# A gated stage stretched over ten and a half images of a deformable stage, with the preparation of the last images moved and compressed

## Chip, core and metric

The kernel runs on one core of one Trainium2 chip. The metric is the device time of one execution in microseconds (us). Three runs of the kernel before gave a median of 13687.8 us (13683.05 to 13691.02).

## What is computed

The input is 32 images of 128 channels on a 32 x 32 grid, in fp32. Two residual layers follow each other. Cut to what matters:

```python
# layer 0: state-space layer with a gate, on group-normalised x
h = einsum('bdl,de->ble', u, W_enc) + b_enc            # 128 -> 1024 features
y = causal_convolution(h, K) + D * h                   # K has 64 taps per feature
y = gelu(y)
g = y @ W_glu + b_glu                                  # 1024 -> 2048
g = g[..., :1024] * sigmoid(g[..., 1024:])
out = layernorm(h + g) @ W_dec + b_dec                 # 1024 -> 128
x = x + out
# layer 1: deformable 8 x 8 depthwise convolution, on group-normalised x
off = depthwise_conv3x3(x, offset_w) + offset_b        # 64 taps, 2 offsets each
for tap in 64 taps:                                    # bilinear sampling at moved places
    acc += weight[tap] * sample(x, place(tap) + off[tap])
x = x + gelu(batchnorm(acc))
```

The gate `g` of layer 0 and its decoding are called the gated part here, layer 1 the deformable part. An image needs both, in this order.

## The kernel before

`main_block` (L518) runs after the convolution of layer 0, whose result for all images lies in DRAM. It is a list of instructions written out in order for every engine: under `tc.manual_schedule()` each engine and each DMA queue works through its own list in the order in which the Python code issues the instructions.

**Gated part.** `first_part(b)` (L718) is a generator. For each image it runs two halves of 512 columns; in each half, for each of eight feature blocks m, TensorE makes the gate (L729, eight matmuls), the value (L752, eight) and the residual `gph` (L768, one), and decodes the block before it (L657). It yields 863 after every matmul, 292 times an image. ScalarE (ACT) takes the gate out of PSUM with a sigmoid (L736) and squares the result (L789); VectorE (DVE) adds bias and multiplies (L760, L781); GpSimd (POOL) sums (L659, L790). `close` (L674) spreads the layer norm of a half over the next fifteen yields, by `later` and `tick`, and ends with the store of the image's half to `x1_d`. Gate, value and residual share three PSUM buffers.

**Deformable part.** `second_part(b)` (L1039) runs 17 packs of columns, each in four pieces; a piece has three matmuls `dps` (L1063), so an image has 204. The count of an image's matmuls, 0 to 203, is called its slot here. DVE takes each matmul out of PSUM times the weights (L1066, four PSUM buffers); POOL adds the product up (L1077, L1082). The matmul's moving operand is `ds` times `dhy` (L1020 in `weights`, two pieces ahead). Both are loaded from DRAM by the SyncE (SP) queue (`load_hat`, L988, up to five and six pieces ahead), out of tables of "hats" max(0, 1 - |rel - k|). For the last two images (`ALONE = B - 2`) only a quarter of each `ds` is loaded, and ACT copies it to the other partitions (L1012 in `spread_fine`, three pieces ahead); DVE also takes half of the first additions from POOL there (L1077).

**Preparation.** `prepare(b)` (L805) returns the steps that make the tables of image b, each with the slot of image b - 1 at which `second_part` issues it: `fetch` 28 (SP loads the stored `x1_d`), `total` 35, `mean` 37, `variance` 40 and `normal` 42 (group norm, with two small matmuls in TensorE's list and a square root on ACT), nine `taps` of the 3 x 3 convolution at 44 to 68 on DVE, `turn` 47 and 50 (transposes), `largest` 71, `across` 74 and `down` 79 on DVE, `spread` 81 and 82 (eight SP DMAs each to a DRAM scratch), `gather` 89 and 90 (an SP load back, each), and 24 `hat` steps from 96 to 174: two ACT activations (L925, L926) on one of two `hat` buffers and a store of 312 KB from ACT's queue (L927). `ready` at 178 only makes the tables known to Python. The first load of the next image's tables is issued at slot 186.

**Order.** `run_along` (L505) merges generators so that they advance in proportion to the totals given with them: it always takes the next item of the one whose share of its total is smallest. Gated image b + 2 is merged with deformable image b for b = 0 to 29; deformable images 30 and 31 have no gated part beside them.

Of the kernel before, what the change touches and what calls it, by code (L numbers as in the profile page):

```python
# [15 lines left out]
B, C, H, W = 32, 128, 32, 32  # L16
# [445 lines left out]
PIECES = 8 // KY2  # L462
# [15 lines left out]
def span_of(u):  # L478

    j0, j1 = max(0, 7 - u), min(7, NU - 1 - u) + 1  # L480
    return j0, j1 - j0


def rows_of(piece):

    a, b = 15 - KY2 * piece, 23 - KY2 * piece
    return (0, a), (a, b - a), (b, H - b)
# [17 lines left out]
def run_along(*streams):  # L505


    left = [[gen, float(total), 0.0] for gen, total in streams]
    while left:
        s = min(left, key=lambda e: e[2] / e[1])  # L510
        cost = next(s[0], None)
        if cost is None:
            left.remove(s)
        else:
            s[2] += cost


def main_block(nc, tc, const, ins, x, u_d, y_d, x1_d, out, offmax):  # L518
# [16 lines left out]
    T = 512  # L535
    YB = 11
    ALONE = B - 2
    SB, HB = 5, 4
    ctx = ExitStack()
    with ctx:  # L540
# [55 lines left out]
        for k in range(KD):  # L596
            nc.tensor.matmul(
                fold[:, 0:1], w_dec[:, k, :], beta[:, k : k + 1],
                start=(k == 0), stop=(k == KD - 1),
# [19 lines left out]
        for i in range(2):  # L619
            t = dram1.tile([2, NCOL], F32, tag=f"rel_d{i}", name=f"rel_d{i}")  # L620
            flat = t.rearrange("a (p l) -> (a p) l", p=P // 2)
            n = 2 * NCOL // P
# [177 lines left out]
        FIRST = 2 * (KD * (2 * KD + 2) + 2) * MM  # L800
# [1 line left out]

        images = {}

        def prepare(b):  # L805

            st = {}

# [34 lines left out]
            def taps(lo, hi):  # L843
                def run():
                    if lo == 0:
                        st["co"] = two.tile([P, L], F32, tag="img", name=f"dco_{b}")
                    co3 = st["co"].rearrange("p (h w) -> p h w", w=W)
                    v3 = st["v"].rearrange("p (h w) -> p h w", w=W)
                    for n in (4, 0, 1, 2, 3, 5, 6, 7, 8)[lo:hi]:
                        dy, dx = n // 3 - 1, n % 3 - 1  # L850
                        y0, y1 = max(0, -dy), H - max(0, dy)
                        x0, x1 = max(0, -dx), W - max(0, dx)
                        src = v3[:, y0 + dy : y1 + dy, x0 + dx : x1 + dx]
                        to = co3[:, y0:y1, x0:x1]
                        wn = off_w[:, n : n + 1]
                        if n == 4:
                            nc.vector.tensor_scalar(
                                to, src, wn, off_b, op0=ALU.mult, op1=ALU.add
                            )
                        else:  # L860
                            nc.vector.scalar_tensor_tensor(
                                to, src, wn, to, op0=ALU.mult, op1=ALU.add
                            )

                return run
# [88 lines left out]
            def ready():  # L954
                images[b] = st["vt_d"], [st["h0"], st["h1"]]

            steps = [
                (28, fetch), (35, total), (37, mean), (40, variance), (42, normal),
                *((44 + 3 * i, taps(i, i + 1)) for i in range(9)),
                (47, turn(0)), (50, turn(1)),  # L960
                (71, largest), (74, across), (79, down), (81, spread(0)), (82, spread(1)),
                (89, gather(0)), (90, gather(1)),
                *((96 + 82 * i // len(hats), step) for i, step in enumerate(hats)),
                (178, ready),
            ]
            return steps

        NP = len(PACKS)
        pieces = [(b, n, i) for b in range(B) for n in range(NP) for i in range(PIECES)]
# [2 lines left out]
        def slots_of(n):  # L972
            return sum(span_of(u)[1] for u in PACKS[n][1])

        def runs_of(n):

            runs, slot = [], 0
            for u in PACKS[n][1]:
                j0, nj = span_of(u)
                first = u * 8 + j0  # L980
                if runs and first == runs[-1][0] + runs[-1][2]:
                    runs[-1][2] += nj
                else:
                    runs.append([first, slot, nj])
                slot += nj
            return runs

        def load_hat(k, a):  # L988
# [7 lines left out]
            else:  # L996
                t = hy_of[k] = hypool.tile([P, 16, KY2, H], F32, tag="hy", name=f"dhy_{k}")
            rows = 4 if a == 0 and b >= ALONE else 16
            for first, slot, m in runs_of(n):
# [6 lines left out]
        def spread_fine(k):  # L1006

            if k >= len(pieces) or pieces[k][0] < ALONE:
                return
# [13 lines left out]
        def windows(b, n):  # L1023

            if n == NP:
                b, n = b + 1, 0
            x0 = PACKS[n][0]
            if b == B or (n > 0 and PACKS[n - 1][0] == x0):
                return
            t = xw_of[b, x0] = three.tile(  # L1030
                [P, len(YWINDOWS), C], F32, tag="xw", name=f"dxw_{b}_{x0}"
            )
            for j, y0 in enumerate(YWINDOWS):
                nc.sync.dma_start(
                    t[:, j, :],
                    at(images[b][0], (y0 * W + x0) * C, [[W * C, 16], [C, 8], [1, C]]),
                )

        def second_part(b, steps):  # L1039


            steps = sorted([*steps, *ending], key=lambda e: e[0])
            ending.clear()
            acc = one.tile([P, W, H], F32, tag="acc", name=f"dacc_{b}")
            nc.gpsimd.memset(acc, 0.0)
            for n in range(NP):
                x0, us = PACKS[n]
                m = slots_of(n)
                xw = xw_of[b, x0]
                windows(b, n + 1)  # L1050
                for i in range(PIECES):
                    k = (b * NP + n) * PIECES + i
                    s = s_of.pop(k)
                    w = wk[:, table_of[n] : table_of[n] + m, KY2 * i : KY2 * (i + 1)]
                    prod = ppool.tile([P, 16, KY2, H], F32, tag="prod", name=f"dp_{k}")
                    for j, (y0, ny) in enumerate(rows_of(i)):
                        while steps and steps[0][0] <= 3 * (PIECES * n + i) + j:
                            steps.pop(0)[1]()
                        ps = psam.tile([P, 512], F32, tag="sam", name=f"dps_{k}_{j}")
                        ps = ps[:, : m * KY2 * ny].rearrange(  # L1060
                            "p (s k y) -> p s k y", s=m, k=KY2
                        )
                        nc.tensor.matmul(  # L1063
                            ps, xw[:, j, :], s[:, :m, :, y0 : y0 + ny], start=True, stop=True
                        )
                        nc.vector.tensor_mul(  # L1066
                            prod[:, :m, :, y0 : y0 + ny],
                            ps,
                            w[:, :, :, None].to_broadcast([P, m, KY2, ny]),
                        )  # L1070
                        if j == 0:
                            weights(k + 2)
                            spread_fine(k + 3)
                        yield measure(m * KY2 * ny)
                    load_hat(k + SB, 0)
                    adder = nc.vector if b >= ALONE and i % 2 else nc.gpsimd
                    adder.tensor_add(prod[:, :m, 0], prod[:, :m, 0], prod[:, :m, 1])  # L1077
                    slot = 0
                    for u in us:
                        j0, nj = span_of(u)  # L1080
                        to = acc[:, u - 7 + j0 : u - 7 + j0 + nj]
                        nc.gpsimd.tensor_add(to, to, prod[:, slot : slot + nj, 0])  # L1082
                        slot += nj

            o = two.tile([P, L], F32, tag="img", name=f"do_{b}")
            xr = two.tile([P, L], F32, tag="img", name=f"dxr_{b}")
            nc.sync.dma_start(xr, x1_d[b])
            nc.gpsimd.tensor_scalar(
                o.rearrange("p (h w) -> p w h", w=W), acc, bn_mean, bn_inv,
                op0=ALU.subtract, op1=ALU.mult,  # L1090
            )
            ending.append((6, lambda: nc.scalar.activation(o, o, AF.Gelu, bias=bn_beta)))
            ending.append((11, lambda: nc.vector.tensor_add(o, o, xr)))
            ending.append((14, lambda: nc.scalar.dma_start(out[b], o)))

        ending = []
        def measure(columns):

            return columns + 40.0

        SECOND = sum(
            measure(slots_of(n) * KY2 * ny)
            for n in range(NP) for i in range(PIECES) for _, ny in rows_of(i)
        )
# [16 lines left out]
        ctx.enter_context(tc.manual_schedule())  # L1121
        run_along((first_part(0), FIRST))
        run_along((first_part(1), FIRST), (opening(), 90.0))
        for b in range(B):
            steps = prepare(b + 1) if b + 1 < B else []
            if b + 2 < B:
                run_along(
                    (first_part(b + 2, last=(b + 2 == B - 1)), FIRST),
                    (second_part(b, steps), SECOND),
                )  # L1130
            else:
                run_along((second_part(b, steps), SECOND))
        for _, step in ending:
            step()

# [148 lines left out]
```

## Time and profile before

| what | value |
|---|---|
| median of three runs | 13687.8 us |
| the profiled execution, its own time | 13693.54 us |
| its span, from first to last instruction | 13691.8 us |
| PE busy in the span | 13161.7 us (96%) |
| DVE, POOL, ACT busy | 8807.4 (64%), 9028.9 (66%), 3285.6 us (24%) |
| gated image 0 with nothing beside it | 251.0 us (1577.9 to 1828.9) |
| a deformable image with a gated one beside it | 368.1 us |
| deformable image 30, alone, with the preparation of image 31 | 295.6 us (13139.4 to 13435.0) |
| deformable image 31, alone, with the tail of the kernel | 256.8 us (13435.0 to 13691.8) |

Image boundaries are read from the timeline: a gated image begins with its first L729, a deformable one with the clearing of its accumulator on POOL (L1045). Gated image 31 has its last L729 at 13113.1 us.

The busy shares are means over the whole span. They say little of a single stage, so the stages are asked one by one, with the stretches of the table as windows. A line of such an answer gives the stretch, its length and, for each engine, the busy time and the number of instructions in it, then the granted TensorE clock, the mean busy share of the DMA engines and GB/s.

### The profile page before, as it was taken

To read this page: it belongs to the slowest core of one execution; us is meant where nothing else is said; L and a number is where in the kernel's file an instruction comes from. 1 tells how busy PE (TensorE), PEld (TensorE's weight loads), DVE (VectorE), ACT (ScalarE), POOL (GpSimd) and SP (SyncE) were. 2 spreads that over 40 slices of the span, in tenths; PEclk is the share of its full clock that TensorE was granted. 3 is DMA by queue.
4 is the path that set the end of the run, shared out by engine and by line. 5 is a ranking of instruction groups with operands and counts; after the bars stand their busy time and mean duration, and the time that the engine had idled before them with its cause. 6 is when DMAs were issued, how large, how long until landed. Compare 5 with 4: busy or idle time off the path is not lost.

```text
span 13691.8 us, 134306 instructions
## 1 busy us (share of the span) xinstructions
PE 13161.7 (96%) x40482; PEld 7261.4 (53%) x40482; DVE 8807.4 (64%) x12719; ACT 3285.6 (24%) x4767; POOL 9028.9 (66%) x8834
## 2 busy tenths in 40 slices
PE   7889899999999999999999999999999999999976
PEld 6888645555555555555555555555555555555533
DVE  6777426666666666666666666666666666666677
ACT  4333222121112222222222121222222222222245
POOL 2444216777777777777777777777777777777766
PEclk8999999999999999999999999999999999999988
DMA  6888518888888888888888888888888888888865
GB/s 222 265 259 264 181 57 222 233 230 229 230 233 234 240 235 234 234 233 229 238 239 233 230 230 231 232 232 241 236 234 236 231 231 235 239 237 229 230 197 166
DMA packets 1715628, 3105.79 MB, mean 227 GB/s; under 512 B 308306, under 2 KB 1018322, under 8 KB 1713874
## 3 DMA queue, kind: packets, MB, share of 16 engines
q1 hardware_dynamic: 1502290, 2641.91, 71.9%
q10 hardware_dynamic: 163456, 320.92, 6.5%
q0 software_dynamic: 49152, 134.28, 3.0%
q8 instruction: 329, 5.39, 0.2%
q14 instruction: 401, 3.28, 0.1%
HBM read 2630.36 MB, written 466.06 MB: 226 GB/s over the span
## 4 chain that ended last, share of the span: by engine, by line
PE 80%; DMA 10%; DVE 4%; ACT 2%; POOL 2%; issue 1%; SPq 1%; ACTq 0%; DVEq 0%; POOLq 0%
PE gpv L752 24%; PE gpg L729 24%; PE dps L1063 23%; DMA ds<-dhat 4%; PE gph L768 3%; DMA y_d<-yo 3%; PE gpo L657 3%; PE psz L224 3%; DVE z L231 2%; PE psy L270 2%; DMA dhat<-dh 1%; DVE ds L1020 1%; POOL y_d L303 1%; ACT ds L1012 1%; DMA dhy<-dhat 1%
## 5 line engine op out<-in xcount | busy, mean ns | idle before, releaser
L1066 DVE TENSOR_TENSOR dp<-dps,k_weight_slots 128x256 f32<-128x256 f32 (+17 forms) x6528 | 3081.4, 482 | 3051.3 <-PE dps L1063 2869.6
L1063 PE MATMUL dps<-ds,dxw 128*128 128x256 f32 (+18 forms) x13056 | 4729.4, 448 | 208.3 <-DVE dp L1066 197.6
L1082 POOL TENSOR_TENSOR dacc<-dacc,dp 128x256 f32<-128x256 f32 (+3 forms) x4736 | 4415.1, 932 | 443.2 <-DVE dp L1077 75.6
L1063 PEld LDWEIGHTS dps<-ds,dxw 128*128 128x128 f32 x13056 | 2472.7, 193 | 3221.1 <-issue 2578.0
L729 PE MATMUL gpg<-gy,g_w_glu 128*128 128x512 f32 x8192 | 3987.7, 593 | 22.5 <-DMA gy<-y_d 15.8
L752 PE MATMUL gpv<-gy,g_w_glu 128*128 128x512 f32 x8192 | 3974.5, 592 | 0.0
L1077 POOL TENSOR_TENSOR dp<-dp 128x512 f32<-128x512 f32 (+3 forms) x2108 | 2621.5, 1244 | 1909.4 <-DVE dp L1066 1906.7
L1020 DVE TENSOR_TENSOR ds<-ds,dhy 128x1024 f32<-128x1024 f32 (+3 forms) x2176 | 3152.6, 1449 | 810.9 <-DMA ds<-dhat 659.2
L729 PEld LDWEIGHTS gpg<-gy,g_w_glu 128*128 128x128 f32 x8192 | 1544.7, 190 | 1238.2 <-issue 966.7
L752 PEld LDWEIGHTS gpv<-gy,g_w_glu 128*128 128x128 f32 x8192 | 1548.7, 189 | 1158.3 <-issue 915.4
L790 POOL TENSOR_TENSOR gs<-gs,gq 128x512 f32<-128x512 f32 x448 | 633.8, 1415 | 1343.7 <-ACT gq L789 1343.7
L789 ACT ACTIVATE gq<-gr 128x512 f32<-128x512 f32 x448 | 282.2, 630 | 4648.5 <-DVE gr L781 4564.7
L303 POOL DMA_DIRECT2D y_d<-yo x1024 | 590.5, 584 | 949.4 <-ACT yo L291 820.9
L736 ACT ACTIVATE gs<-gpg,k_b_glu 128x512 f32<-128x512 f32 x512 | 351.9, 687 | 2490.0 <-PE gpg L729 2355.6
L270 PE MATMUL psy<-toe,z 128*128 128x192 f32 x4096 | 718.3, 335 | 102.0 <-ACT yo L291 100.2
L925 ACT ACTIVATE dh<-dr,k_minus 128x624 f32<-128x624 f32 x768 | 621.7, 810 | 648.3 <-DMA dhat<-dh 569.8
L270 PEld LDWEIGHTS psy<-toe,z 128*128 128x128 f32 x4096 | 675.1, 193 | 144.4 <-ACT yo L291 138.9
L282 DVE TENSOR_TENSOR psy<-psy,t 32x256 f32<-32x256 f32 (+1 forms) x1280 | 554.1, 433 | 272.9 <-ACT t L278 241.1
L760 DVE SCALAR_TENSOR_TENSOR gs<-gpv,k_b_glu,gs 128x512 f32<-128x512 f32 x512 | 379.9, 742 | 437.4 <-PE gpv L752 423.5
L224 PE MATMUL psz<-w_enc,u 128*128 128x128 f32 x4096 | 576.8, 296 | 86.4 <-DVE z L231 40.2
L659 POOL TENSOR_TENSOR gs<-gs,gr 128x512 f32<-128x512 f32 x448 | 634.9, 1417 | 0.0
L926 ACT ACTIVATE dh<-dh,one 128x624 f32<-128x624 f32 x768 | 626.2, 815 | 24.9
(162 smaller groups left out, 6091.4 us busy)
## 6 DMA issues: line engine op xcount, KB each, us to landing
dhy<-dhat SPq DMA_DIRECT2D x1536, 512.0 KB
ds<-dhat SPq DMA_DIRECT2D x1440, 512.0 KB
dhat<-dh ACTq DMA_DIRECT2D x768, 312.0 KB
y_d<-yo POOLq DMA_DIRECT2D x1024, 128.0 KB, 5.0
gy<-y_d SPq DMA_DIRECT2D x512, 256.0 KB
u<-u_d SPq DMA_DIRECT2D x224, 512.0 KB
toe<-kp_d SPq DMA_DIRECT2D x128, 768.0 KB
dxw<-dvt_d SPq DMA_DIRECT2D x1248, 64.0 KB
```

The costliest lines, as they stand in the source:

```text
L224: nc.tensor.matmul(ps[:, j, :], u[:, (NB * g + ORDER[j]) * P : (NB * g + ORDER[j] + 1) * P], w_enc[:, k * P : (k + 1) * P], start=True, st ...
L270: nc.tensor.matmul(ps[:, c // 2, c % 2, :], rows[i][:, g * CG + c0 + c, :], toe[:, c0 + c, :], start=True, stop=True,)
L303: nc.gpsimd.dma_start(y_d[d0 : d0 + CG, :, i * NB + ORDER[j], :].rearrange("d b l -> b d l"), yo[i][j * B : (j + 1) * B],)
L659: nc.gpsimd.tensor_add(sums[0], sums[0], r)
L729: nc.tensor.matmul(gate, w_glu[:, k, D + m * P : D + m * P + P], ys[k], start=(k == 0), stop=(k == KD - 1),)
L752: nc.tensor.matmul(val, w_glu[:, k, m * P : m * P + P], ys[k], start=(k == 0), stop=(k == KD - 1),)
L790: nc.gpsimd.tensor_add(sums[1], sums[1], sq)
L1020: nc.vector.tensor_mul(s[:, :m], s[:, :m], hy[:, :m])
L1063: nc.tensor.matmul(ps, xw[:, j, :], s[:, :m, :, y0 : y0 + ny], start=True, stop=True)
L1066: nc.vector.tensor_mul(prod[:, :m, :, y0 : y0 + ny], ps, w[:, :, :, None].to_broadcast([P, m, KY2, ny]),)
L1077: adder.tensor_add(prod[:, :m, 0], prod[:, :m, 0], prod[:, :m, 1])
L1082: nc.gpsimd.tensor_add(to, to, prod[:, slot : slot + nj, 0])
```

## The change

Up to deformable image 19 the order stays as it is, but that the `ready` step, which issues nothing, stands at 184 and not at 178. From deformable image 20 on the ten gated images 22 to 31 are one generator, the deformable images 20 to 31 another, and they are merged so that the ten gated images last as long as ten and a half deformable ones. Gated image b + 2 therefore ends 0.05 images later for each image from 20 on, and gated image 31 ends in the middle of deformable image 30. The preparation of image b + 1 starts later by the same amount, and its steps are drawn together so that they still end at slot 184: of the distance from 184 a step keeps (184 - start) / 156, from 1 for image 21 to 0.346 (start 130) for image 31.

```diff
+    SLOWER = B - 12
+    LONGER = 0.5
+    FETCH, READY = 28, 184
...
-        def prepare(b):
+        def prepare(b, start=FETCH):
...
-                (178, ready),
+                (READY, ready),
             ]
-            return steps
+            stretch = (READY - start) / (READY - FETCH)
+            return [(READY - int((READY - n) * stretch), step) for n, step in steps]
...
-        for b in range(B):
-            steps = prepare(b + 1) if b + 1 < B else []
-            if b + 2 < B:
-                run_along(
-                    (first_part(b + 2, last=(b + 2 == B - 1)), FIRST),
-                    (second_part(b, steps), SECOND),
-                )
-            else:
-                run_along((second_part(b, steps), SECOND))
+        for b in range(SLOWER):
+            run_along(
+                (first_part(b + 2), FIRST), (second_part(b, prepare(b + 1)), SECOND)
+            )
+        n = B - 2 - SLOWER
+        pace = (n + LONGER) / n
+        def firsts():
+            for b in range(SLOWER + 2, B):
+                yield from first_part(b, last=(b == B - 1))
+        def seconds():
+            for b in range(SLOWER, B):
+                steps = []
+                if b + 1 < B:
+                    done = (b - SLOWER) * (pace - 1)
+                    steps = prepare(b + 1, FETCH + int(3 * NP * PIECES * done))
+                yield from second_part(b, steps)
+        run_along((firsts(), n * FIRST), (seconds(), (n + LONGER) * SECOND))
```

More of the change, by code (lines that the diff above doesn't have):

```diff
@@ L957, in prepare @@
             steps = [
-                (28, fetch), (35, total), (37, mean), (40, variance), (42, normal),
+                (FETCH, fetch), (35, total), (37, mean), (40, variance), (42, normal),
                 *((44 + 3 * i, taps(i, i + 1)) for i in range(9)),
```

## The prediction, made before the changed kernel ran

> **What bounds the kernel now.** I read the stages first, because the shares of the whole span hide the end. This is the answer for the gated image 0 alone, deformable image 28 beside gated image 30, the hand-over, and the two images alone.
>
> ```profile
> core 0: us, PE busy (x) PEld busy (x) DVE busy (x) ACT busy (x) POOL busy (x), PEclk, DMA share, GB/s
> 1577.90:1828.90 251.00, 251.00 (x579) 111.00 (x580) 29.30 (x39) 26.24 (x37) 32.36 (x26) 0.99 0.08 28
> 12403.10:12770.50 367.40, 366.17 (x1006) 187.69 (x1005) 235.89 (x336) 77.04 (x103) 266.78 (x246) 1.00 0.87 235
> 13117.70:13139.40 21.70, 16.93 (x39) 8.10 (x37) 9.71 (x14) 7.60 (x9) 15.65 (x17) 0.84 0.33 106
> 13139.40:13435.00 295.60, 192.31 (x427) 94.21 (x428) 225.04 (x331) 183.02 (x197) 183.80 (x185) 0.75 0.64 186
> 13435.00:13691.80 256.80, 158.87 (x397) 79.39 (x395) 210.62 (x307) 130.36 (x131) 189.70 (x184) 0.84 0.58 168
> ```
>
> A merged image is PE from end to end (366.2 of 367.4), so it costs the gated 251.0 plus what the 204 `dps` matmuls need, 368.1 - 251.0 = 117.1 us. Alone, an image takes 256.8 or 295.6 us: there PE waits. The waits of image 30 say for whom, and the costliest groups of that stretch say what ACT and DVE do.
>
> ```profile
> PE dps L1063 <- DVE dp L1066: 88.5, 75, 3.7
> ACT ds L1012 <- DMA ds<-dhat: 86.4, 39, 7.5
> DVE ds L1020 <- ACT ds L1012: 62.9, 39, 5.5
> PE gn_pm L824 <- ACT dv L820: 6.1, 1, 6.1
> ```
>
> ```profile
> L1012 ACT COPY ds<-ds 32x1024 f32<-32x1024 f32 (+7 forms) x138 | 136.2, 987 | 113.2 <-DMA ds<-dhat 86.4 <-PE dps L1063 11.4 <-ACT dh L926 7.5
> L1020 DVE TENSOR_TENSOR ds<-ds,dhy 128x1024 f32<-128x1024 f32 (+3 forms) x70 | 99.1, 1416 | 65.2 <-ACT ds L1012 62.9 <-DMA ds<-dhat 2.2
> ```
>
> PE waits for DVE, and DVE in turn, 62.9 us of image 30, for ACT's copies. In the middle of image 31, with no preparation, DVE is busy nearly without a gap (31.8 of 32.1 us), and a pack takes 14.2 us in its timeline, 1.18 us a slot. In image 30 ACT is nearly full while it makes hats, as its timeline shows: a copy pair of 2.1 us, a hat of 1.6, its issue of 0.33.
>
> ```profile
> 13340.81 0.81 ACT L926 ACTIVATE dh<-dh,one 128x624 f32<-128x624 f32 x1
> 13341.66 0.33 ACTq L927 DMA_DIRECT2D dhat<-dh  x1
> 13342.02 2.12 ACT L1012 COPY ds<-ds 32x1024 f32<-32x1024 f32 x2 [0.40 <-ACT dh L926]
> 13344.17 0.82 ACT L925 ACTIVATE dh<-dr,k_minus 128x624 f32<-128x624 f32 x1
> ```
>
> The other long step is the spread, seen in the SP queue's timeline of image 30:
>
> ```profile
> 13254.21 4.73 SPq L896 DMA_DIRECT2D rel_d<-drel  x8
> ...
> 13259.61 4.36 SPq L896 DMA_DIRECT2D rel_d<-drel  x8
> ...
> 13268.66 0.59 SPq L910 DMA_DIRECT2D dr<-rel_d  x1
> ```
>
> **What the Trainium skill says.** "DMA: Bandwidth & Descriptors", section "Issuing engines are not separate DMA queues": transfers of SP, ACT and POOL run on the same 16 DMA engines and interleave. The trace agrees: in the packets of ACT's queue the last one of a hat ends mostly 1.8 us after the issue in the opening, beside gated image 1, but 2.9 to 6.5 in image 30 and 2.2 to 8.2 in image 25, beside SP's loads. "Perfetto Trace Analysis", section "DMA Instruction — HWDGE (DVE, Sync)": the profiled interval ends when the sequencer is free, the movement is not in it. It agrees too: 0.33 us for L927 against those 1.8 to 8.2. "ScalarE: Activation LUTs", section "What ACT_TABLE_LOAD costs": about 1283 ns a load; the load ahead of the square root (L835) took 1.28 us.
>
> **The change part by part.** The sum is a difference against the profiled execution (13693.5 us, its span 13691.8 and 1.7 around it); I add it to the median, 13687.8, 5.7 below that execution.
>
> *Merged stage.* The gated work is the same. Ten gated images now carry 10.5 deformable ones: 0.5 x 117.1 = **+58.6**. The half image 30 in it brings ACT copies (34 x 2.1 us) and 17 additions of 0.74 us on DVE, in about 184 us where ACT was busy about 38 and DVE about 118: they lie beside PE. If that cover failed, the DVE part would cost at most 12.6.
>
> *Image 30 alone.* Before, image 29's last product was at 13125.5 and image 31's first at 13428.0; less a normal gap of 2.4 that is **-300.1**. It includes about 14 us in which `close` of gated image 31 ran with nothing beside it (DVE waited 6.7 for `gm`, then worked its chain). After, slots 102 to 203 remain: packs 8.5 to 15 at image 31's rate 107.3, the last pack at image 30's own 23.2 (four short runs per table, where SP issues 8 loads of 0.65 us for a piece of 3.6 us), 130.5; and `close`, now between pieces, at DVE's own 7.0 plus a wait, 8. Then the preparation P, wholly in this half, slots 130 to 184:
>
> - DVE work: `normal` 1.3, taps 11.7, `largest` 1.2, `across` 2.1, `down` 1.7, 18.0 in a stage that DVE bounds.
> - The norm chain, `fetch` 130, `total` 133, `mean` 134, `variance` and `normal` 135. Before there were 14 slots. PE stands at `gn_pm` for ACT (6.1 above), with all `dps` behind it, ACT at the fetch, with the copies behind it, and DVE at the square root and its table load. About 6 of DVE idle, 3 more than before.
> - Spread and gather: 16 issues on SP, 10 us, the gather's landing about 16 us after `down`. In slots that is 149 to 154, 6 us. Behind them on SP stand the `ds` and `dhy` loads, behind the waiting hat on ACT the copies. DVE can go on to slot 159 from copies already made, so 5 or 6 us are lost.
> - Hats: slots 154 to 181 hold 24 hats and 9 copy pairs. A hat needs 2.07 us of ACT (back to back in the opening), so 24 x 2.07 + 9 x 2.12 = 69 us, in a stretch of 27 slots, 32 us. From `down` to slot 183: 16 + 69 = 85 against 35 x 1.18 = 41, so 44 with the gather's loss. The buffers are two, so a store landing after 4.5 us makes (2.07 + 4.5) / 2 = 3.3 a hat, 79 in all: +10. SP catches up meanwhile with the last pack's loads, -4. I take 43.
>
> P = 18 + 6 + 43 = **67**. From below: no landing waits, chain at 2, SP's catch-up 8: 53. From above: all stores land late and the chain costs 10: 82. Sum: 130.5 + 8 + 67 = **+205.5**.
>
> *Preparation of images 22 to 30, merged.* A slot is 1.83 us. `ready` costs nothing; all that moves is ACT, DVE, PE and SP items, past each other's neighbours, and what matters is who stands behind. The order of the built kernel has, for image 30's preparation (slots 119 to 184), 12 hats between one gate sigmoid and the next and 10 in the next gap. A gate comes every 23 us; 12 hats need 25 us of ACT with no landing wait, about 35 at 2.9 each. The lag grows to about 26 us. Behind it stand sigmoid and square; the gate's PSUM is needed again after the value's matmuls, 11 us later, and DVE's four buffers and POOL's products give about 4 more. Some 8 us lost, in image 29. The norm chain, taps squeezed from 24 to 10 slots (DVE 60% busy plus 12 us in 18) and the spread with a gather after three slots instead of eight add about 5. Images 28 and 27 are milder (hats every 2.9 and 3.3 us): 3 and 1. Earlier ones keep over 3.6 us a hat: zero. **+17**. From below: such steps already cost about 2 us of PE an image (19.5 of 21.7 in one window of image 25), where the loads of `gy` meet the gather; the shift may part them, -10 in all. From above: 45.
>
> Sum: 58.6 - 300.1 + 205.5 + 17 = **-19**, 13669. Image 31 stays at 256.8, POOL tail included.
>
> **Rivals.**
> - *The squeeze is hidden.* P 55 and no loss in the merged images: 58.6 - 300.1 + 193.5 = -48, **13640**. For it: POOL and DVE have 30% to spare there and the waits named are short. Against: in image 30 the hats and copies alone are 69 us of ACT in 32. Chance 0.30.
> - *A jam at ACT makes it slower.* In image 25 hat stores land after 5 to 8 us beside full loads; two buffers then give 4.5 us a hat, 108 us instead of 59 for image 30's hats. Lag 49, less 15 of slack: 34 lost; for images 29, 28, 27 in the same way 23, 13, 3, and 13 for chains and gathers: 86, so -36 + 86 = +50, **13738**. Place: sigmoids of gated images 29 to 31. It decides from 36 us of loss on. For it: ACT already waits 17 us an image for these stores. Against: the DMA engines are less loaded in packs 12 to 16 (share 0.56 to 0.8), and a stalled PE asks for fewer loads. Chance 0.13.
> - The change does what it says: the built order has the last gated matmul in image 30's middle and image 31's `fetch` after the store.
>
> **Numbers.** The forecast case has 0.57. It covers 13652 to 13690, and about a fifth of it, 0.11, lies below 13660. A measurement of this kernel can tell about 0.2%, 27 us, from no change. Faster: 0.30 + 0.11 = 0.41; within: 0.47; slower: 0.12. All low ends together give 58.6 - 300.1 + 138.5 + 53 - 10 = -60, all high ones 58.6 - 300.1 + 138.5 + 82 + 45 = +24. They will hardly all meet, so the range stops a few us short of both: -53 to +20, 13635 to 13708; the upper end reaches into the jam.
>
> **What would show it.** After: image 30's middle to image 31's first product about 205 us; ACT over 90% busy for 70 us there, L1020 waiting for L1012; merged images 20 to 25 at 374 us each with PE full; in image 29 sigmoids late behind L925, PE idle some 13 us. It is wrong if the hats of image 30 take 100 us, or if PE idles in images 26 to 28.

## The result, and the profile after

The changed kernel takes 13801.5 us (median of four runs, 13796.9 to 13812.6) against 13689.4 for the kernel before in the same comparison. The ratio is 1.0083, with a 95% interval of 1.0066 to 1.0101: it is slower by 112 us. The forecast was 13669, and the range to 13708 misses the time by 93.

The profiled execution took 13796.91 us, its span 13795.1, which is 103.3 more than the span before. Lines have moved by three to five: `dps` L1063 is now L1068, its eviction L1066 is L1071, the copies L1012 are L1017, the hats L925 to L927 are L929 to L931, the sigmoid L736 is L739.

The same table of stages as before (stretch, length, busy time of PE, PEld, DVE, ACT and POOL, the granted clock, DMA share, GB/s), for the deformable images 28 and 29, the first and the second half of image 30, and image 31:

```profile
core 0: us, PE busy (x) PEld busy (x) DVE busy (x) ACT busy (x) POOL busy (x), PEclk, DMA share, GB/s
12364.00:12754.10 390.10, 361.45 (x970) 185.10 (x969) 234.36 (x331) 75.30 (x100) 269.13 (x250) 0.96 0.84 223
12754.10:13139.80 385.70, 365.54 (x984) 187.19 (x983) 232.94 (x331) 80.27 (x103) 261.25 (x236) 0.97 0.81 219
13139.80:13329.20 189.40, 180.85 (x485) 92.44 (x484) 118.59 (x179) 87.20 (x96) 119.84 (x119) 0.97 0.48 131
13329.20:13531.00 201.80, 107.14 (x221) 53.45 (x220) 122.09 (x176) 110.89 (x124) 84.99 (x87) 0.65 0.54 155
13531.00:13795.10 264.10, 159.59 (x405) 79.50 (x403) 214.05 (x313) 134.10 (x135) 197.17 (x189) 0.85 0.58 167
```

Image boundaries here, and in all tables below, are the first eviction L1071 of an image in the timeline. Two things are to be seen. The second half of image 30 took 201.8 us, near the 205.5 of the forecast. And a merged image is no longer PE from end to end: in image 28 PE stood idle 390.10 - 361.45 = 28.7 us, and its clock was 0.96, not 1.00. All that was lost was lost in the merged stage:

| stage | forecast | measured |
|---|---|---|
| image 20 to slot 102 of image 30 | 3682.2 + 58.6 + 17 = 3757.8 | 9440.7 to 13329.2 = 3888.5 |
| slots 102 to 203 of image 30 | 205.5 | 201.7 |
| image 31 (before: 263.9 counted in this way) | unchanged | 264.2 |

The 3682.2 is the kernel before in the same count, from 9445.7, the start of image 20, to 13127.9, image 29's last product and a normal gap. So the merged stage is 131 over the forecast, the half image 4 under it.

**Where it went, seen from PE.** These are windows over images 20 to 29 as a whole, first of the kernel before, then of the changed one:

```profile
9437.00:13133.00 3696.00, 3668.36 (x10064) 1882.33 (x10063) 2387.78 (x3358) 776.49 (x1027) 2675.52 (x2471) 1.00 0.86 233
```

```profile
9440.70:13139.80 3699.10, 3581.53 (x9768) 1840.96 (x9767) 2357.07 (x3326) 777.14 (x1014) 2681.25 (x2442) 0.99 0.86 232
```

The two stretches are equally long, but in the second a twentieth of the gated work of every image has been pushed out into image 30. PE's idle time rose from 27.6 to 117.6 us. And the records of the granted clock show 99.0 us at half speed, in 18 stretches, where before there were 2.1 us, at the very end of the window. PE stood idle in a part of these 99.0 us; in 73.7 of them it worked, at half speed, so about 37 us of work was lost.

**Who made PE wait.** The waits of images 20 to 29 (engine, waiting line, what it waited for: us in total, times, longest), before:

```profile
POOL gs L790 <- ACT gq L789: 293.4, 131, 5.4
...
ACT dh L925 <- DMA dhat<-dh: 189.0, 68, 7.8
...
DVE dp L1066 <- POOL dacc L1082: 35.1, 22, 2.4
...
PE dps L1063 <- DVE dp L1066: 13.2, 20, 1.9
```

and after:

```profile
POOL gs L793 <- ACT gq L792: 440.5, 117, 23.7
ACT dh L929 <- DMA dhat<-dh: 359.0, 136, 6.9
...
ACT dh L929 <- DMA dr<-rel_d: 138.2, 9, 23.8
DVE dp L1071 <- POOL dacc L1087: 105.6, 49, 11.3
...
PE dps L1068 <- DVE dp L1071: 30.1, 20, 4.7
...
PE gpg L732 <- DMA gy<-y_d: 29.3, 13, 8.0
...
PE gpg L732 <- ACT gs L739: 24.6, 9, 7.0
...
PE gn_pm L828 <- ACT dv L824: 18.1, 3, 9.1
```

ACT stood 359 us for the stores of hats (189 before) and 138 us for the gather at the head of the hats (not in the list before). ACT is not the bound, and PE's idle time rose by 90 us only, so most of these 497 us cost nothing. What costs is what stands behind: the squares L792, for which POOL now waits up to 23.7 us, DVE behind POOL up to 11.3, and the sigmoid L739. PE's own waits are spread over four things: 30.1 us for DVE to free a `dps` buffer, 29.3 for the columns `gy` of a gated half, 24.6 for the sigmoid and 18.1 for the statistics of the group norm (`gn_pm`). ACT's timeline in image 29 shows one such jam whole:

```profile
13031.73 0.81 ACT L929 ACTIVATE dh<-dr,k_minus 128x624 f32<-128x624 f32 x1 [14.51 <-DMA dr<-rel_d]
...
13033.42 0.33 ACTq L931 DMA_DIRECT2D dhat<-dh  x1
...
13041.86 0.81 ACT L929 ACTIVATE dh<-dr,k_minus 128x624 f32<-128x624 f32 x1 [6.39 <-DMA dhat<-dh]
...
13043.98 0.69 ACT L739 ACTIVATE gs<-gpg,k_b_glu 128x512 f32<-128x512 f32 x1 [0.46 <-ACT dh L930]
```

The first hat waits 14.5 us for the gather. Its store is issued at 13033.42; the third hat needs the same buffer and starts only when that store has landed, at 13041.86, 8.4 us after the issue. The sigmoid comes behind it. PE's timeline of the same time:

```profile
13044.72 2.07 PE L732 MATMUL gpg<-gy,g_w_glu 128*128 128x512 f32 x2 [6.95 <-ACT gs L739]
...
13050.46 1.02 PE L732 MATMUL gpg<-gy,g_w_glu 128*128 128x512 f32 x2
```

and ten microseconds of it as a window:

```profile
13040.00:13050.00 10.00, 5.28 (x9) 2.42 (x10) 4.63 (x7) 3.83 (x5) 1.40 (x1) 0.66 1.03 312
```

PE waits 6.95 us for the sigmoid that frees the gate's PSUM. Then two gate matmuls take 2.07 us, and six microseconds later 1.02: after the gap the clock was at half, and its mean in the window is 0.66 (the records have it at half from 13041.7 to 13048.5, so it fell while PE still stood). The DMA engines are full there (share 1.03).

### The profile page after: what moved, and what is told of

It reads as the page before. It is cut to its first block, busy times and chain, and to the rows that moved or that the text cites. A ratio compares the mean times of both kernels' runs of the same rounds, so it can differ in the third digit from the quotient of the medians.

```text
span 13795.1 us, 134284 instructions
## 1 busy us (share of the span) xinstructions
PE 13175.0 (96%) x40482; PEld 7271.4 (53%) x40482; DVE 8800.7 (64%) x12719; ACT 3302.5 (24%) x4776; POOL 9056.3 (66%) x8834
## 5 line engine op out<-in xcount | busy, mean ns | idle before, releaser
L1071 DVE TENSOR_TENSOR dp<-dps,k_weight_slots 128x256 f32<-128x256 f32 (+17 forms) x6528 | 3080.5, 483 | 3111.2 <-PE dps L1068 2845.5
L1068 PE MATMUL dps<-ds,dxw 128*128 128x256 f32 (+18 forms) x13056 | 4730.0, 448 | 219.5 <-DVE dp L1071 216.0
L1068 PEld LDWEIGHTS dps<-ds,dxw 128*128 128x128 f32 x13056 | 2476.3, 193 | 3250.8 <-issue 2610.9
L1082 POOL TENSOR_TENSOR dp<-dp 128x512 f32<-128x512 f32 (+3 forms) x2108 | 2700.9, 1281 | 1769.7 <-DVE dp L1071 1767.2
L792 ACT ACTIVATE gq<-gr 128x512 f32<-128x512 f32 x448 | 282.2, 630 | 4547.1 <-DVE gr L784 4487.5
L739 ACT ACTIVATE gs<-gpg,k_b_glu 128x512 f32<-128x512 f32 x512 | 351.9, 687 | 2334.8 <-PE gpg L732 2151.9
L929 ACT ACTIVATE dh<-dr,k_minus 128x624 f32<-128x624 f32 x768 | 622.3, 810 | 964.5 <-DMA dhat<-dh 751.8
```

The costliest lines, as they stand in the source:

```text
L929: nc.scalar.activation(t, st["t", a], AF.Abs, bias=minus[:, k : k + 1])
L1068: nc.tensor.matmul(ps, xw[:, j, :], s[:, :m, :, y0 : y0 + ny], start=True, stop=True)
L1071: nc.vector.tensor_mul(prod[:, :m, :, y0 : y0 + ny], ps, w[:, :, :, None].to_broadcast([P, m, KY2, ny]),)
```

## The experiments

Two theories stood against each other after the result. The *squeeze theory*: the compressed preparations cost PE its time, not the stretching. The *pace theory*: a gated image stretched over 1.05 deformable ones makes waits of its own, whatever the preparation does. Within the first came the question of which part of the compressed preparation: the stores of the hats (landing), the chain of the group norm (fetch), the gather, or the meeting of the gated part's half ends with the preparation (meeting).

### Either half of the change alone

The compressed preparations in the old one-to-one order, image 31's at its old place:

```diff
-                    done = (b - SLOWER) * (pace - 1)
+                    done = (b - SLOWER) * (pace - 1) if b < ALONE else 0.0
-        run_along((firsts(), n * FIRST), (seconds(), (n + LONGER) * SECOND))
+        run_along((firsts(), n * FIRST), (seconds(), n * SECOND))
```

> The merging goes one to one, as before, but the preparation of images 22 to 30 stands at the slots of the changed kernel (image 31's as before). Squeeze theory (the compressed preparation stalls the merged images): deformable images 24 to 29 each take 8 to 35 us more than 368, some 90 to 130 us in all, time 13780 to 13820. Pace theory (the denser deformable work beside each gated image overloads DMA and SP, with the preparation where it was or not): at most 20 us more than before, 13690 to 13710. Meeting theory (the loads of gy at the end of a gated half, which drifts through the image, meet spread and gather): those ends stay at slots 102 and 204 here, so images 24 and 25 lose almost nothing and only the late sigmoids of 27 to 29 remain, 13720 to 13750.

Measured, one run: 13810.4 us, against 13682.9 for the kernel before on that chip. Images 20 to 29 took 3812.5 us where the kernel before had 3696.1: +116. PE was idle for 111 us in them (31 before, with the same boundaries) and worked for 76 us at half clock, which lost about 38. The squeeze costs this much without any stretching.

The stretching without the preparations of images 22 to 30 (these images use image 21's tables):

```diff
-                    steps = prepare(b + 1, FETCH + int(3 * NP * PIECES * done))
+                    if SLOWER < b < ALONE:
+                        images[b + 1] = images[SLOWER + 1]
+                    else:
+                        steps = prepare(b + 1, FETCH + int(3 * NP * PIECES * done))
```

> The merging of the changed kernel, without the preparation of images 22 to 30 (they use image 21's tables, so that part of the computation is left out); image 31 is prepared as in the changed kernel. Squeeze theory: merged images 21 to 29 take 356 us each, 10.5 of them 3740, image 30's second half as in the changed kernel, time 13640 to 13670. Pace theory: they still take 364 us or more each, and the time stays above 13720. Meeting theory: as the squeeze theory, since there is no spread or gather to meet.

Measured, one run: 13630.3 us. Images 20 to 29 as a whole, and one image of them:

```profile
9438.00:12966.00 3528.00, 3521.33 (x9659) 1817.92 (x9658) 2210.76 (x3203) 369.01 (x489) 2627.45 (x2446) 1.00 0.84 218
...
11562.30:11913.80 351.50, 351.50 (x965) 181.56 (x964) 220.69 (x319) 33.17 (x44) 261.61 (x245) 1.00 0.84 216
```

PE is idle for 6.7 us in ten images, with POOL and the loads of tables nearly as they were: the pace theory falls. It also gives the true length of a merged image without preparation, 351.5 us, where my division of the gated and the deformable work gave 3740.8 / 10.5 = 356.3. The difference, 4.8 an image, was by this working preparation too, and was there already before.

Taken together: to slot 102 of image 30 this kernel needs 3716.8 us, the changed one 3888.5. The preparations merged with gated work thus cost 172 us; the forecast had 17 + (3740.8 - 3716.8) = 41. Over images 20 to 29 alone it is 3699.1 - 3527.7 = 171, of which 117.6 - 6.7 = 111 are idle PE and about 35 work lost to half clock ((73.7 - 3.4) / 2). The remaining 25 are about what the preparations' own matmuls take, 28 us in the records; these do not come from the squeeze.

### The stores of the hats

Four `hat` buffers, not two:

```diff
-        spool, hypool, hatpool = pool("mbs", SB), pool("mbh", HB), pool("mbq", 2)
+        spool, hypool, hatpool = pool("mbs", SB), pool("mbh", HB), pool("mbq", 4)
```

> The changed kernel with four hat buffers instead of two. If the landing of the hats' stores, at two buffers, is what makes ACT late (the forecast's rival): ACT's waits of L929 for dhat fall from 188 us in images 25 to 30 to under 60, and 50 to 110 us come back, 13690 to 13750. If the wait for the gather and ACT's own work at hats make it late, or loads that arrive late: under 30 us come back, 13770 to 13800.

Measured, one run: 13696.9 us. The waits of images 20 to 29:

```profile
POOL gs L793 <- ACT gq L792: 355.6, 119, 15.0
...
ACT dh L929 <- DMA dr<-rel_d: 141.4, 9, 24.6
...
DVE dp L1071 <- POOL dacc L1087: 46.2, 33, 8.9
...
ACT dh L929 <- DMA dhat<-dh: 40.1, 21, 3.8
```

The wait for landing went from 359.0 to 40.1 us, the merged stage from 3888.5 to 3807.2, PE's idle time to 60.7 us and the half-clock time to 51.2. The wait for the gather stayed. Of PE's own waits, those for `dps` buffers, `gy` and the sigmoid fell (to 16.1, 7.2 and 9.5 us), and that for the statistics did not (22.6). The same kernel with more runs:

> The changed kernel with four hat buffers again, timed in rounds (the first look gave 13697): by the landing theory 13685 to 13710, so still not faster than before, and 20 to 45 us over the kernel before with four buffers (13667), which is what the squeeze costs without the two buffers' wait.

Measured: 13688.1 us (12 runs), ratio to the kernel before 0.9999 [0.9990, 1.0008]. The landing theory holds: 113 us of the change's time come back, and what is left is a kernel as fast as the one before. Not all of the 113 is the merged stage. The two profiled executions, 84 and 100 us shorter than that of the changed kernel, have 73 and 81 there, 8 and 7 in the half image, and 5 and 13 up to image 20, whose preparations also have the buffers. So I asked what the buffers bring without the change. The same edit on the kernel before:

> The kernel before with four hat buffers. Landing theory (two buffers make ACT wait for the hats' stores, and how much that costs depends on how close the hats stand): with hats 6 us apart there is little to win, the 1 us an image that the changed kernel with four buffers shows in its unchanged images 1 to 19, so 13650 to 13675. If four buffers give as much here as in the changed kernel (over 80 us), the squeeze was not what made them matter: under 13610.

Measured: 13666.6 us (21 runs), 0.9983 [0.9976, 0.9989]. Images 20 to 29 gain only 10 us (3685.7) although the wait for landing falls from 189.0 to 3.8 us: where hats are spread out, waiting for their stores was nearly free. Against this kernel the change with four buffers is slower by 21.

Leaving the stores out altogether shows what even four buffers leave (images 22 to 30 use image 21's hats, and that part of the computation is missing):

```diff
-                    nc.scalar.dma_start(
-                        at(st[f"h{a}"], k * NCOL, [[HSUB, P], [1, HSUB]]), t
-                    )
+                    if not SLOWER + 1 < b < B - 1:
+                        nc.scalar.dma_start(
+                            at(st[f"h{a}"], k * NCOL, [[HSUB, P], [1, HSUB]]), t
+                        )
```

> The changed kernel with two hat buffers, but the hats of images 22 to 30 are not stored (these images use image 21's tables, so that part is left out); all of ACT's work stays. If the wait for the landing is the cost: images 20 to 29 last 3620 us together, as with four buffers (3699 in the changed kernel), time 13690 to 13710. If the stores' load on the DMA engines costs too: under 3600 and 13680. If ACT's own work were the cost: over 3680.

Measured: 13694.9 us, one run; images 20 to 29 3596.8, the merged stage 3786.0 (two buffers: 3888.5, four: 3807.2). Idle PE is still 46.9 us. So the stores are 102 of the 172 us, their load on the DMA engines included, and four buffers take away 73 to 81. About 69 us lie elsewhere, some 25 of them the preparations' own matmuls. The expectation is met only in part: the time fits the wait for landing alone, images 20 to 29, under 3600, fit a cost of the load as well.

### The squeeze alone, with four buffers

```diff
# on the kernel with the squeeze alone
-        spool, hypool, hatpool = pool("mbs", SB), pool("mbh", HB), pool("mbq", 2)
+        spool, hypool, hatpool = pool("mbs", SB), pool("mbh", HB), pool("mbq", 4)
```

> The squeezed slots in the one-to-one order (as e1_squeeze_alone), with four hat buffers. Landing theory: of the 116 us by which images 20 to 29 were longer than before, 70 to 85 go, as they did in the stretched order (79): 13700 to 13730. If the squeeze costs by ACT's own work or the gather's wait: at most 40 go, 13745 or more.

Measured: 13744.1 us (5 runs), 1.0040 [1.0026, 1.0054], above what the landing theory gave and at the edge of the other reading (13745 or more). Images 20 to 29 took 3764.5 us: 48 back of the 116, and 79 more than the kernel before with four buffers (3685.7). ACT's wait for landing was down to 25.0 us, so the rest is not that wait. In this order PE stood 25.6 us at `gn_pm` (L828) for the statistics on ACT, three times, in images 27 to 29, and the trace has more gaps at slots 105 to 122 of images 21 to 24, where a gated half ends. Whether the stretching, which shifts the half ends against the preparation, makes the same steps cheaper was not tried singly. By the four buffers the landing theory is thus right for somewhat less than half of the loss in both orders, 48 of 116 us and 73 to 81 of 172.

### The norm chain and the gather

With four buffers, the chain `fetch`, `total`, `mean`, `variance`, `normal` of the last preparations gets three slots more for its load to land, and the steps after `normal` stand where they stood or just behind it:

```diff
+            placed = [(READY - int((READY - n) * stretch), step) for n, step in steps]
+            if stretch > 0.6:
+                return placed
+            norm = placed[4][0] + 3
+            return [
+                (n + 3 * (i in (1, 2, 3, 4)) if i < 5 else max(n, norm + 1), step)
+                for i, (n, step) in enumerate(placed)
+            ]
```

> The changed kernel with four hat buffers, and in images 27 to 31 the norm steps after the fetch three slots later. If PE's gaps at gn_pm (7.3, 9.6 and 5.6 us in images 27 to 29 with four buffers) are the fetch's landing, they go, and with them some us of half clock: 13665 to 13685, against 13697 with four buffers alone. If PE only waits elsewhere instead, since the taps then stand closer: within 8 us of 13697.

Measured: 13678.7 us (20 runs), 0.9990 [0.9984, 0.9997]; images 27 to 29 took 1100 us where they had 1113, and PE's wait at `gn_pm` fell from 22.6 to 8.6 us. The medians put the chain at 9 us, the images and the wait at 13 to 14. The intervals of the two kernels overlap, so it is the wait that shows the cost, not the time.

The gather: hats of compressed preparations begin eight slots after the gather and are spread evenly to the old last slot.

```diff
+            first = max(n for n, step in placed if step in gathers) + 8
+            last = placed[-2][0]
+            count = len(hats)
+            return [p for p in placed if p[1] not in hats] + [
+                (first + (last - first) * i // (count - 1), step)
+                for i, step in enumerate(hats)
+            ]
```

> The changed kernel with four hat buffers, and in images 22 to 31 the first hat eight slots after the gather (three to six before), the last one where it was. If ACT standing at the first hat for the gather (141 us in nine images at four buffers) is what is left of the loss, those waits fall under 40 us and images 20 to 29 end 15 to 40 us sooner than with four buffers alone (3620 to 3627): 13650 to 13675. If that wait is idle time that costs nothing, or the hats, standing closer, give it back: within 10 us of 3624, 13680 to 13700.

Measured: 13702.4 us (20 runs), 1.0009 [1.0002, 1.0016]; images 20 to 29 took 3617.6, against 3620 to 3627 with four buffers alone. ACT's wait for the gather was halved, from 141.4 to 75.2 us, and nothing came of it: PE's idle time was 65 us, where it had been 61 and 67. The longest DMA wait of ACT with four buffers could be halved without gain. The gather theory falls as far as this run tried it: 75 us of the wait stayed, and hats that stand closer may have taken back what was won.

### Less stretching

A quarter of an image, two buffers:

```diff
-    LONGER = 0.5
+    LONGER = 0.25
```

> The changed kernel with a stretch of a quarter of an image. The fetch of image 30 then stands at slot 73 (0.71 of the stretch is left) and image 31's at 79. By the squeeze theory the loss is that of the changed kernel's images at the same compression (1.0 to 0.71: 1 to 13 us each in images 20 to 24, 29 in all), plus that of the second half at half of it, and the gain of the end is 0.25 x 117 = 29 given, 60 less in image 30 and 6 from the close that is no longer alone: 13690 - 37 + 35 = 13690, 13670 to 13720. By the pace theory the loss halves, with half the density: 13690 - 37 + 75 = 13730.

Measured: 13732.0 us (6 runs), 1.0032 [1.0020, 1.0045]. The squeeze theory had given 13670 to 13720, so it misses here. The pace theory's 13730 is met, but the run without the preparations leaves that theory no ground; the agreement is one of the number alone. The compression is milder, and yet images 20 to 29 need 3675.1 us. The waits name a part that I had not costed:

```profile
PE gpg L732 <- DMA gy<-y_d: 37.8, 12, 5.8
```

In images 22 to 29 the first gate matmul of a gated half waits 2 to 6 us for its columns: the half's end falls where the preparation keeps SP. The same with four buffers:

> The stretch of a quarter of an image, with four hat buffers. Landing theory alone: the merged images come close to the clean 357 us and most of the 49 us over the kernel before come back and more, 13640 to 13660. Meeting theory (PE's gaps there stand before the first gate matmul of a half, for gy): four buffers do not bring gy sooner, only 15 to 35 us come back, 13690 to 13715.

Measured: 13684.4 us (13 runs), 0.9997 [0.9988, 1.0005], 48 less than with two, between what the landing theory and the meeting theory gave, and nearer to the second. PE's wait for `gy` fell from 37.8 to 22.8 us, so most of it stayed. Both have a part.

### A version that beats both

A quarter of an image, four buffers, but only over the last two gated images, or over the last four:

```diff
-    SLOWER = B - 12
-    LONGER = 0.5
+    SLOWER = B - 4
+    LONGER = 0.25
...
-        spool, hypool, hatpool = pool("mbs", SB), pool("mbh", HB), pool("mbq", 2)
+        spool, hypool, hatpool = pool("mbs", SB), pool("mbh", HB), pool("mbq", 4)
```

> Four hat buffers, a stretch of a quarter of an image over the last two gated images alone (deformable images 28 and 29 run 1.125 times as dense). If a squeezed or shifted preparation is what costs, only images 29 and 30 lose (5 to 10 us each), and against the kernel before with four buffers (13667) the end gives about 20: 13650 to 13665. If the density loads the DMA engines (share 0.94 by the sum of their work, 0.86 before), images 28 and 29 take over 350 us each instead of 336 and it ends at 13675 or more.

> The same quarter over the last four gated images (1.0625 times as dense). Four images with a shifted preparation lose 3 to 8 us each, beside an end that gives about 20: 13655 to 13675. If the shift costs nothing at four buffers: under 13650. If the gated halves' ends, wherever they fall, are what costs, between e9_last_two and e6_quarter_four (13684).

Measured: 13653.9 us (8 runs), 0.9974 [0.9964, 0.9985] for the last two, 13657.1 (19 runs), 0.9978 [0.9971, 0.9985] for the last four (`SLOWER = B - 6`). Both are faster than either kernel, and each lies where its first reading had it. Of the 37 us, 24 are the buffers' (the kernel before with four). The other 13 come from medians of two chips, and the intervals of the two ratios overlap, so that the order alone gains anything is likely, not shown. With the quarter over two, the last half of image 30 takes 168.5 us, not 201.7, as image 31's preparation is compressed less, and a single merged image, 29, carries a compressed preparation.

## Why the prediction was wrong

**What bounds the kernel.** Right: PE in the merged stage, and DVE with ACT's copies behind it in image 30.

**Merged stage, +58.6.** The sign and the cover were right (the image without preparation has PE full), the term a little large. Against 3682.2 the stage without merged preparations is at 3716.8, +34.6: 24 us of what I put down to `dps` was the preparation, which I had inside the 368.1 of an image and did not see as a cost.

**Image 30 alone, -300.1 + 205.5.** Right: 201.7 for the second half. Its waits:

```profile
PE dps L1068 <- DVE dp L1071: 83.3, 35, 8.4
DVE ds L1025 <- ACT ds L1017: 71.2, 15, 9.4
...
ACT ds L1017 <- DMA ds<-dhat: 51.5, 16, 14.2
...
ACT dh L929 <- DMA dhat<-dh: 10.9, 8, 3.1
```

PE waits for DVE and DVE for ACT's copies, as forecast. The 24 hats ran from 13426.2 to 13500.2, 74 us, where I had 69 to 79. One detail was off: I said ACT would be over 90% busy in that time, and it was busy 54.8 of 74.0, since it stood there for stores and for loads of `ds`. That 201.7 falls so near to 205.5 is in part luck: the terms given for the hats, 44 + 10 - 4, make 50 and not the 43 taken, and with 50 the half would have been put at 212.5. Its parts, the packs, `close` and the preparation, were not measured singly.

**Preparation of images 22 to 30, merged, +17. This step failed.** With the 24 us named above the forecast held 41; it measured 172. Its parts:

- *The hats behind one sigmoid.* "12 hats need 25 us of ACT with no landing wait, about 35 at 2.9 each." The rate was a little low: the first of image 29's hats started at 13031.7 and the last at 13108.3, 3.3 each. The slack was wrong. I let 15 us of lag go free behind ACT and counted the lag from the first hat at its slot. But the first hat waits for the gather, 14.5 us in image 29, so the slack is used up before the hats start. At the sigmoid itself PE stood 6.95 us, near the 8 forecast, and 20 us in image 29 as a whole, where I had some 13. POOL stands up to 23.7 us for a late square. And I followed one queue only: DVE behind POOL (105.6 us, 35.1 before) came in as a second path to PE. Stores in all: 102 us, by the kernel without them.
- *"Earlier ones keep over 3.6 us a hat: zero."* They were not zero. Above the clean 351.5 the changed kernel's images cost, in us:

| image | 20 | 21 | 22 | 23 | 24 | 25 | 26 | 27 | 28 | 29 |
|---|---|---|---|---|---|---|---|---|---|---|
| above 351.5 | 5.5 | 11.3 | 9.7 | 7.9 | 17.9 | 12.7 | 18.5 | 27.8 | 38.5 | 34.3 |

  The first four have 8.6 on average, where an image had carried about 4.8 before. Images 24 to 26 have 13 to 19 each, though the hats stood over 3.6 us apart there. The loads of `gy` at a half's end are among it (29.3 us in the waits of all ten).
- *"The norm chain, taps ... and the spread with a gather ... add about 5."* The chain alone was worth some 9 to 14.
- *Not in the sum at all:* the clock. I priced a stall of PE at its own length. Here 111 us more of stalls brought some 35 us of work lost at the lower clock with them.

**The rivals.** "A jam at ACT makes it slower" is what happened, in its place (the sigmoids of gated images 29 to 31 late behind hats) and for the larger part by its mechanism, stores that land late in two buffers: 102 of the 172 us. It was to decide from 36 us of loss on; in the forecast's own terms the loss was 17 + 131 = 148. It gave 13738, with 34, 23, 13 and 3 us lost in images 29 to 26; measured above the clean image are 34, 39, 28 and 19, and a good part lies in earlier images, where it had nothing. I gave it 0.13, on two grounds: that the DMA engines are less loaded in the late packs, and that a stalled PE asks for fewer loads. The window at 13040, inside those packs, speaks against both: the DMA engines were full while PE stood. "The squeeze is hidden" was wrong by all of these 148 us.

**What would make it wrong.** I had written "if PE idles in images 26 to 28"; in image 28 it did, by 28.7 us. One sign was put wrongly: "merged images 20 to 25 at 374 us each" is the length of a gated image by the forecast's sum (3740.8 / 10), a deformable one would have 356; they took 357 to 369. The sign to look for in images 26 to 28 was well chosen, and the profile of before held the ground for it: 68 waits of ACT for stores, up to 7.8 us long, with hats still 82 / 24 = 3.4 slots apart.

**Open.** Of the 172 us the runs put 102 on the stores and some 9 to 14 on the chain, and about 25 are the preparations' own matmuls; the remaining 30 or so no run splits. With four buffers the trace shows gaps before the first gate matmul of a half, gaps of `dps` behind DVE and POOL, and some 19 us of work lost to half clock, but which step of the preparation sets them off was not tried singly.

## What to carry to other kernels

Before steps are drawn together on an engine that works through its list in order, count for each the longest thing it may wait for, a store's landing or a gather, and put it against the slack of what stands behind; the engine's busy share (here 24%) showed nothing of this. Buffers of a store have to last for its landing time under load, not in a quiet stage: two more of 312 KB gave back 113 us of the changed kernel, and 24 of the kernel before. And compress as few images as the end needs: with the same four buffers a quarter over two images was faster than a quarter over ten by 30 us, and than a half over ten by 34.

## What the runs showed of the hardware

A stall of TensorE costs more than its length. The Trainium skill, "TensorE: Matmul & The Clock Gate", section "HAM oscillation — how this bites in real kernels", gives as the rule that no idle gap of PE should be over about 3.4 us, as the clock falls to half behind it. The trace agrees for long gaps and is stricter for short ones. In images 20 to 29 of the changed kernel all 12 gaps over 3.4 us were followed by half clock; behind one of 6.95 us a pair of gate matmuls took 2.07 us, later 1.02. But so were 6 of the 11 gaps of 1.9 to 3.4 us, and none of the 24 gaps of 0.3 to 1.9. The 18 stretches at half clock lasted 3.41, 6.83 or 10.24 us each, 99.0 in all, of which PE worked for 73.7. So the stalls of this kernel cost about 1.3 times their own length, (117.6 + 73.7 / 2) / 117.6. With four buffers and 60.7 us idle, PE worked for 38.5 us at half clock, and the factor is the same. In images 1 to 28 of the kernel before, 63 us of idle PE brought 6.8 us at half clock, in two stretches, behind gaps of 1.9 and 2.6 us.

A hat's store of 312 KB, whose last packet in the opening ended mostly 1.8 us after the issue (2.2 us up to the semaphore that tells of its landing), landed 8.4 us after it in image 29, with the DMA share at 1.03 from 13030 to 13050.
